# A metaformer on one core: which engine empties PSUM in the spectral stage, where its forward transform stands, and how the inverse over blocks is laid out

## The chip, the core and the metric

The kernel runs on one core of a Trainium2 chip. The core's engines work in parallel and are joined by semaphores: TensorE (PE, which multiplies matrices and loads its weights in a row of its own, PEld), VectorE (DVE), ScalarE (ACT), GpSimd (POOL) and SyncE (SP), which issues all DMAs of this kernel. TensorE writes to PSUM, a small memory; DVE or ACT must copy results from there to SBUF, the on-chip working memory, before the PSUM tile can be filled again. The metric is the device time of one execution in microseconds (us).

## The reference, cut to what matters

The model has two layers. Layer 0 is a selective scan in four directions and a soft mixture of experts, layer 1 a sum over rows and columns and a spectral filter. Only the end of layer 1, the spectral filter, is touched by the change.

```python
x = x + _L0_conv_ref(_ln_c(x), ...)            # selective scan, 4 directions
t = t + _L0_ffn_ref(_ln_t(t), ...)             # experts
x = x + _L1_conv_ref(_ln_c(x), Wself, Wm, Wk)
t = t + _L1_ffn_ref(_ln_t(t), sigma, phi, M_u, M_phi_plus, M_phi_minus, log_weights, gumbel)

def _stu_conv(phi, u, n):                      # n = 8192, u: (4, 4096, 128), phi: (4096, 16)
    Vf = jnp.fft.rfft(phi, n=n, axis=0)
    Uf_p = jnp.fft.rfft(u, n=n, axis=1)
    Uf_m = jnp.fft.rfft(u * sgn3, n=n, axis=1)
    U_plus = jnp.fft.irfft(Vf[None, :, :, None] * Uf_p[:, :, None, :], n=n, axis=1)[:, :sl]
    U_minus = jnp.fft.irfft(Vf[None, :, :, None] * Uf_m[:, :, None, :], n=n, axis=1)[:, :sl]
    return U_plus, U_minus * sgn[None, :, None, None]

out = jnp.einsum('btkd,k,kde->bte', U_plus, s, Mpp)
out = out + jnp.einsum('btkd,k,kde->bte', U_minus, s, Mpm)
```

The filter is a causal convolution of each of the 128 channels with 16 filters, followed by a mixing of channels; per frequency this is one 128 x 128 complex matrix, made from the 16 filters' spectra. The result is scaled by a weight per segment of the sequence and added to x.

## The kernel before

**Stages.** `tile_metaformer_kernel` runs a long main phase (the scans, with the other work dealt out between them), then the last experts, and then in sequence `to_slots(B - 1)`, `spectrum()` and `endings()`. The change lies in the last two, with small parts in the constants (`_dft_constants`) and in `filters`.

**The transform in two levels.** The sequence of 4096 is cut into NB = 64 blocks of BP = 64. A first transform over the blocks (`to_slots`) leaves NQ = 64 slots q in the memory tensor `ud`. `spectrum()` works on slots, FB = 2 of them in each of n = 32 rounds, and leaves `zd`, laid out [q, r, p, b, c] with r for real and imaginary part, p the place in the block and b the batch. `endings()` takes the inverse over the blocks and adds it to the residual, `x3_d`.

**One round of `spectrum()`.** Its parts, in the program's words:

- `load(i)` fetches the filters' spectra `vt`, the slots `u1` and the twiddle factors `fq`. `load_back(i)` fetches the product's result of the round before from memory (`zq`) with factors `gq`.
- `forward(i)`, line 1468: for each of the two slots, four matmuls into one half of a PSUM tile (L1474), then one copy of that half to `ut`.
- `taps_of(i)`, line 1486, the making: 16 steps j. Each fills two PSUM tiles of two banks with eight matmuls (L1495) on four row groups of 32, and copies each tile to `wt`, a tile that exists only once (`bufs=1`) (L1506 and L1509).
- `product(i)`, line 1513: 128 matmuls of `wt` with `ut` (L1524), eight PSUM tiles, eight copies to `zs`, which DMAs carry to `zf` in memory.
- `backward(i)`, line 1553: four matmuls of `zq` with `gq` (L1559), one copy to `zo`, two DMAs to `zd`.

All parts take their PSUM tiles from one pool of four (`banks()`), each of two banks. The loop over rounds is:

```python
forward(0)
for i in range(n):
    if i + 2 < n: load(i + 2)
    if i + 1 < n: between[0] = lambda: forward(i + 1)
    if i >= 1:    load_back(i - 1); between[C // 8 - 1] = lambda: backward(i - 1)
    taps_of(i, between)
    product(i)
```

So the forward of the next round stands behind step 0 of a making, the backward of the last behind step 15. An engine's instructions run in the order in which the build leaves them; near the seams of a round the build interleaves neighbouring parts (making instructions stand between the two halves of a forward, and a `zs` copy of the product may stand behind the first `wt` copy).

**Who copies.** `copy()` and `out()` (L1451, L1455) give every copy from PSUM in turn to ACT and DVE, by a counter that runs through all rounds. A round has 43 copies: 32 of `wt`, 2 of `ut`, 8 of `zs`, 1 of `zo`. As 43 is odd, the first copy of a making is ACT's in one round and DVE's in the next.

**`endings()`.** 16 groups g of four places p. `load_x` brings x3 into `xr3`, [64 blocks, 4 places, batch, channel], one DMA for each batch entry; `load` brings `zb`, [128, 4, 512], in two DMAs of 64 partitions; `turn` has four matmuls with the constant `gi_t` (128 x 64) into [64, 512] of PSUM (L1612), and for each a DVE operation that multiplies by `wpj`, the weight of the block's segment, and adds x3 (L1614); `put` writes the group to the output by four DMAs. All are issued by SP in the order of the program's text, with four groups of x3 fetched ahead. `wpj` is made in `filters` from a table of segments, on 64 partitions.

Of the kernel before, what the change touches and what calls it, by code (L numbers as in the profile page):

```python
# [47 lines left out]
def _dft_constants():  # L48


    j, q = np.arange(NB)[:, None], np.arange(NQ)[None, :]
    th = 2 * np.pi / (2 * NB) * (j * q)
    one = (q == 0) & (j >= 0)
    alt = np.where(j % 2 == 0, 1.0, -1.0) * np.ones((1, NQ))
    co, si = np.cos(th), np.sin(th)
    fwd = np.stack([co, np.where(one, alt, -si)], 1)
    back = np.stack([np.where(one, 1.0, 2 * co), np.where(one, alt, -2 * si)], 1) / (2 * NB)
    gi = np.moveaxis(back, 0, 2)

    seg = np.zeros((NB, 4))  # L60
    for i in range(NB):
        seg[i, 0 if i < NB // 8 else 1 if i < NB // 4 else 2 if i < NB // 2 else 3] = 1.0
    r = fwd.reshape(NB, 2 * NQ), gi.reshape(2 * NQ, NB), seg
    return [np.ascontiguousarray(x.astype(np.float32)) for x in r]


# [35 lines left out]
def kernel(  # L102
# [115 lines left out]
    gq_d = nc.inline_tensor(gq_c, name="dft_out").ap()  # L218
    fu_t = wp.tile([NB, P], F32, name="fu_t")
    nc.sync.dma_start(fu_t, nc.inline_tensor(fu_c, name="dft_u").ap())  # L220
    gi_t = const.tile([P, NB], F32, name="gi_t")
    nc.sync.dma_start(gi_t, nc.inline_tensor(gi_c, name="dft_back").ap())
    wpj = const.tile([NB, 1], F32, name="wpj")

    eps5 = wp.tile([P, 1], F32, name="eps5")
    nc.vector.memset(eps5, 1e-5)
# [477 lines left out]
    def filters():  # L704

        with tc.tile_pool(name="fl", bufs=2) as fp:
# [30 lines left out]
            for s in range(2, -1, -1):  # L737
                nc.vector.tensor_add(
                    wseg[:, s : s + 1], wseg[:, s + 1 : s + 2], wt[:, 3 - s : 4 - s]
                )  # L740
            sg4 = fp.tile([NB, 4], F32, name="sg4")
            nc.sync.dma_start(sg4, nc.inline_tensor(seg_c, name="dft_seg").ap())
            nc.vector.tensor_mul(sg4, sg4, wseg[0:NB, :])
            nc.vector.reduce_sum(wpj, sg4, axis=AX.X)

            nc.scalar.activation(sg, sg, AF.Ln)
# [686 lines left out]
    def spectrum():  # L1433

        with tc.tile_pool(name="sp", bufs=2) as sp, tc.tile_pool(
# [7 lines left out]
                )  # L1443
            wt = sp.tile([P, C // 4, FB * 2 * BP, 4], F32, name="wt", bufs=1)
            u1, fq, vt, ut, zq, gq = {}, {}, {}, {}, {}, {}
            side["e"] = 0

            def banks():
                return sps.tile([P, 2, 512], F32, name="sp_ps", tag="ps")

            def copy():  # L1451
                side["e"] += 1
                return nc.scalar.copy if side["e"] % 2 else nc.vector.tensor_copy

            def out(dst, src):  # L1455
                copy()(dst, src)  # L1456

            def load(i):
                vt[i] = sp.tile([P, FB, 2 * BP], F32, name="vt")
# [8 lines left out]
            def forward(i):  # L1468
                ps = banks()
                ut[i] = sp.tile([P, FB, BP, 2, B], F32, name="ut")  # L1470
                for s in range(FB):
                    q = FB * i + s
                    for b in range(B):
                        nc.tensor.matmul(  # L1474
                            ps[:, s, b * 2 * BP : (b + 1) * 2 * BP],
                            u1[q][:, b, :],
                            fq[q],
                            start=True,
                            stop=True,
                        )  # L1480
                    out(
                        ut[i][:, s].rearrange("d m u b -> d b (m u)"),
                        ps[:, s].rearrange("d (b n) -> d b n", b=B),
                    )

            def taps_of(i, between):
                for j in range(C // 8):
                    pair = [banks(), banks()]
                    for t in range(2):
                        for g in range(4):  # L1490
                            rows = slice(g * KK, (g + 1) * KK)
                            bank = pair[g // 2][:, g % 2]
                            woven = bank.rearrange("d (n t) -> d t n", t=2)[:, t]
                            plain = bank[:, t * 256 : (t + 1) * 256]
                            nc.tensor.matmul(  # L1495
                                woven if (g // 2 + j) % 2 else plain,
                                taps[rows, j, t, :],
                                vt[i][rows].rearrange("k s n -> k (s n)"),
                                start=True,
                                stop=True,  # L1500
                            )
                    for h in range(2):
                        dst = wt[:, 2 * j + h]
                        if (h + j) % 2:
                            src = pair[h].rearrange("d g (n t) -> d n g t", t=2)
                            copy()(dst.rearrange("d n (g t) -> d n g t", g=2), src)  # L1506
                        else:
                            src = pair[h].rearrange("d g (t n) -> d n (g t)", t=2)
                            copy()(dst, src)  # L1509
                    if j in between:  # L1510
                        between[j]()

# [55 lines left out]
            n = NQ // FB  # L1568
            load(0)
            load(1)  # L1570
            forward(0)
            for i in range(n):
                between = {}
                if i + 2 < n:
                    load(i + 2)
                if i + 1 < n:
                    between[0] = lambda: forward(i + 1)
                if i >= 1:
                    load_back(i - 1)
                    between[C // 8 - 1] = lambda: backward(i - 1)  # L1580
# [4 lines left out]

    def endings():

        with tc.tile_pool(name="gi", bufs=3) as gp, tc.tile_pool(
            name="gi_ps", bufs=8, space=PSUM
        ) as gps:  # L1590
            zb, xr = {}, {}

            def mine(t, b, g):
                return t[b].rearrange("(j p) c -> j p c", j=NB)[:, 4 * g : 4 * g + 4, :]

            def load_x(g):
                xr[g] = gp.tile([NB, 4, B, C], F32, name="xr3", bufs=6)
                for b in range(B):
                    nc.sync.dma_start(xr[g][:, :, b, :], mine(x3_d, b, g))  # L1599

            def load(g):
                zb[g] = gp.tile([P, 4, B * C], F32, name="zb", bufs=4)
                for r in range(2):
                    nc.sync.dma_start(
                        zb[g][r * NQ : (r + 1) * NQ],
                        zd[:, r, 4 * g : 4 * g + 4].rearrange("q p b c -> q p (b c)"),
                    )

            def turn(g):
                for t in range(4):  # L1610
                    ps = gps.tile([NB, B * C], F32, name="gi_ps", tag="ps")
                    nc.tensor.matmul(ps, gi_t, zb[g][:, t, :], start=True, stop=True)  # L1612
                    xt = xr[g][:, t].rearrange("j b c -> j (b c)")
                    nc.vector.scalar_tensor_tensor(xt, ps, wpj, xt, ALU.mult, ALU.add)  # L1614

            def put(g):
                for b in range(B):
                    nc.sync.dma_start(mine(out, b, g), xr[g][:, :, b, :])

            for g in range(4):  # L1620
                load_x(g)
            n = BP // 4
            for g in range(n + 3):
                if g + 4 < n:
                    load_x(g + 4)
                if g < n:
                    load(g)
                if 0 <= g - 2 < n:
                    turn(g - 2)
                if 0 <= g - 3 < n:  # L1630
                    put(g - 3)

    def run(pieces):
        for _ in pieces:
# [352 lines left out]
```

## Time and profile before

| What | Time |
|---|---|
| Median of 3 runs | 10265.2 us (10250.67 to 10266.36) |
| The profiled execution itself | 10262.52 us |
| Span of its trace, first to last instruction | 10260.5 us |
| Mean granted TensorE clock | 0.814 of full speed |
| Main phase and last experts, up to the start of `to_slots` | about 8693 us |
| `to_slots`, tables and start of `spectrum()` | about 8693 to 8757 us |
| `spectrum()`, to the issue of its last DMA | to about 10099 us |
| `endings()`, first load to the end | 10101.5 to 10260.5 us |

The profile is of one execution. The page gives each engine's busy time and the costliest groups of instructions over the whole span; the chain of waits is the work that ended last, followed back from the end; the timeline shows instructions in order of time (start, duration, engine, line, operation, how many were merged into the line, and in brackets the idle time of the engine before them and what ended it). Windows give each engine's busy time within a stretch, TensorE's granted clock, the busy share of the 16 DMA engines and the bytes moved per second. A share somewhat above 1 comes from packets that overlap.

### The profile page before, as it was taken

How to read it: one execution, taken by the hardware profiler on the slowest of the kernel's cores; microseconds unless marked ns; L12 is line 12 of the kernel's file. 1: busy time of each engine (PE TensorE's matmuls, PEld its weight loads, DVE VectorE, ACT ScalarE, POOL GpSimd, SP SyncE). 2: the span in 40 equal slices, each digit the busy share in tenths (PEclk: the TensorE clock that was granted, in tenths of full speed). 3: DMA queues.
4: the chain of work that ended last, by engine and by line, in shares of the span. 5: the costliest groups of instructions: out<-in, count | busy, mean ns of one | idle time of the engine just before them, and what ended most of it. 6: DMA issues, size and time to landing. Idle time of an engine off the chain costs nothing. (4 is left out here: it accounts for less than half of the span.)

```text
span 10260.5 us, 137964 instructions
## 1 busy us (share of the span) xinstructions
PE 7621.4 (74%) x45570; PEld 4890.3 (48%) x45570; DVE 8536.1 (83%) x7103; ACT 6160.7 (60%) x11847; POOL 6493.8 (63%) x5948
## 2 busy tenths in 40 slices
PE   7676776667667767677767776767777667899996
PEld 3444444444543545444544554543555445555552
DVE  0899999989999999998999999999999961566663
ACT  4665766656755466676765576765576653455551
POOL 1677787877877778887877788877778751000000
PEclk9788787767877878788868887868877777999998
DMA  2556556657656645656847656856646664333336
GB/s 89 167 172 205 179 182 216 190 180 219 202 167 202 220 154 171 203 182 198 252 163 225 214 158 206 239 161 222 220 158 195 196 183 134 94 88 90 90 89 162
DMA packets 941919, 1806.04 MB, mean 176 GB/s; under 512 B 88184, under 2 KB 506648, under 8 KB 937624
## 3 DMA queue, kind: packets, MB, share of 16 engines
q1 hardware_dynamic: 941208, 1797.22, 56.5%
q8 instruction: 366, 6.00, 0.2%
q14 instruction: 345, 2.83, 0.1%
HBM read 1554.66 MB, written 242.22 MB: 175 GB/s over the span
## 5 line engine op out<-in xcount | busy, mean ns | idle before, releaser
L1846 POOL TENSOR_TENSOR hh<-hh,bc 128x1024 f32<-128x1024 f32 x2048 | 4888.7, 2387 | 387.3 <-DVE hh L1836 152.7
L1836 DVE TENSOR_TENSOR_SCAN hh<-da,hst,db 128x512 f32<-128x512 f32 x3584 | 4392.6, 1267 | 285.3 <-PE y L1872 31.0
L1872 PE MATMUL y<-ident,hh 128*128 128x128 f32 x16384 | 2716.0, 320 | 1530.3 <-POOL hh L1846 1432.6
L1786 ACT ACTIVATE da<-dl,aneg 128x512 f32<-128x512 f32 x4096 | 2783.0, 717 | 1560.3 <-DVE hh L1836 1547.5
L1872 PEld LDWEIGHTS y<-ident,hh 128*128 128x128 f32 x16384 | 2250.2, 165 | 2493.3 <-POOL hh L1846 1867.2
L1830 DVE TENSOR_TENSOR db<-du,bc 128x1024 f32<-128x1024 f32 x1920 | 2365.1, 1232 | 108.3 <-ACT du L1767 28.2
L1845 POOL COPY hst<-hh 128x2 f32<-128x2 f32 x1792 | 365.6, 204 | 1052.9 <-DVE hh L1836 922.0
L1495 PE MATMUL sp_ps<-vt,taps 32*128 32x256 f32 x8192 | 630.5, 409 | 17.9 <-DVE wt L1506 6.3
L1836 DVE TENSOR_TENSOR_SCAN hh<-da,db 128x512 f32<-128x512 f32 x512 | 597.0, 1208 | 38.5 <-PE y L1872 5.8
L440 PE MATMUL cv_ps<-xh,diag 128*128 128x512 f32 x1152 | 525.1, 598 | 1.7 <-ACT sg_v L382 0.9
L1495 PEld LDWEIGHTS sp_ps<-vt,taps 32*128 32x128 f32 x8192 | 426.7, 186 | 204.4 <-DVE wt L1506 78.8
L1524 PE MATMUL sp_ps<-wt,ut 128*32 128x256 f32 x8192 | 448.7, 379 | 1.4 <-DVE wt L1509 1.4
L1830 DVE TENSOR_TENSOR db<-dx,bc 128x1024 f32<-128x1024 f32 x128 | 175.7, 1373 | 298.8 <-POOL dx L1714 287.4
L1686 PE MATMUL dt_ps<-dts,dtw 8*128 8x512 f32 x512 | 380.1, 846 | 51.3 <-ACT sg_v L382 34.5
L1711 PE MATMUL dl_ps<-ex,ident 128*128 128x512 f32 x512 | 321.6, 717 | 127.5 <-POOL ex L1705 127.5
L1506 DVE COPY wt<-sp_ps 128x1024 f32<-128x1024 f32 x256 | 313.3, 1224 | 106.6 <-PE sp_ps L1495 93.1
L1509 DVE COPY wt<-sp_ps 128x1024 f32<-128x1024 f32 x256 | 313.0, 1223 | 79.2 <-PE sp_ps L1495 76.3
L1456 DVE COPY zs<-sp_ps 128x1024 f32<-128x1024 f32 x128 | 156.5, 1222 | 254.2 <-PE sp_ps L1524 252.0
L1705 POOL TENSOR_TENSOR ex<-ex,dx 128x1024 f32<-128x1024 f32 x128 | 301.8, 2358 | 103.9 <-DMA bc<-bc_d 72.9
L1524 PEld LDWEIGHTS sp_ps<-wt,ut 128*32 128x32 f32 x8192 | 264.7, 110 | 193.9 <-issue 23.5
L1509 ACT COPY wt<-sp_ps 128x1024 f32<-128x1024 f32 x256 | 259.1, 1012 | 147.5 <-PE sp_ps L1495 145.5
L1714 POOL TENSOR_TENSOR dx<-dl,xc 128x1024 f32<-128x1024 f32 x128 | 302.5, 2364 | 64.4 <-ACT dl L1712 56.5
(289 smaller groups left out, 9915.7 us busy)
## 6 DMA issues: line engine op xcount, KB each, us to landing
bc<-bc_d SPq DMA_DIRECT2D x2048, 512.0 KB
xc<-xc_d SPq DMA_DIRECT2D x128, 512.0 KB
y_d<-ys SPq DMA_DIRECT2D x128, 512.0 KB
w1t<-in_w_dram SPq DMA_DIRECT2D x96, 512.0 KB
w2t<-in_w_dram SPq DMA_DIRECT2D x192, 256.0 KB
xc_x<-xc_d SPq DMA_DIRECT2D x64, 512.0 KB
yk<-y_d SPq DMA_DIRECT2D x128, 256.0 KB
yk<-y_d SPq DMA_DIRECT2D x256, 128.0 KB
```

The lines of the kernel that those rows point to most:

```text
L440: nc.tensor.matmul(ps, diag[:, h, t, :], xh[:, 8 * g + dy : 8 * g + dy + 8, dx : dx + W], start=(t == 0), stop=(t == 8),)
L1495: nc.tensor.matmul(woven if (g // 2 + j) % 2 else plain, taps[rows, j, t, :], vt[i][rows].rearrange("k s n -> k (s n)"), start=True, stop= ...
L1509: copy()(dst, src)
L1524: nc.tensor.matmul(ps[32 * g : 32 * g + 32, k // 2, (k % 2) * 256 :][:, 0:256], w0.rearrange("d m u b -> d (m u b)"), wt[:, :, n : n + 2, ...
L1686: nc.tensor.matmul(ps, dtw[:, k, h * P : (h + 1) * P], dts, start=True, stop=True)
L1711: nc.tensor.matmul(ps, ident, t[:, h], start=t is dl, stop=t is w)
L1786: i_act = nc.scalar.activation(das[t][:, h, :], sizes[t // N][0][:, h, :], AF.Exp, scale=aneg[:, tk, h, t % N : t % N + 1],)
L1830: nc.vector.tensor_mul(db, src, bcs[s][:, 0:1, :].to_broadcast([P, 2, SC]))
L1836: i_dve = nc.vector.tensor_tensor_scan(o, d0, d1, init, ALU.mult, ALU.add)
L1845: nc.gpsimd.tensor_copy(hsts[t // N][:, :, t % N], hhs[t][:, :, last])
L1846: i_pool = nc.gpsimd.tensor_mul(hhs[t], hhs[t], bcs.pop(t)[:, 1:2, :].to_broadcast([P, 2, SC]))
L1872: i_pe = nc.tensor.matmul(ys[c][:, q, h, :], hhs[t][:, h, q * P : (q + 1) * P], ident, is_transpose=True, start=(n == 0 and k > 0 and q % ...
```

## The change

There are three parts.

1. **Choice of the copying engine.** In place of the counter, `copy(on_act, on_dve)` keeps a running sum of copy times for each engine and gives a copy to ACT if ACT's sum with it is not above DVE's. The times written into the program are 1.01 for ACT and 1.22 for DVE, and 1.06 on both for `ut`. Both sums are set to zero at the start of each round.
2. **Forward in front of the making.** `forward(i + 1)` is called ahead of `taps_of(i)`, no longer behind step 0.
3. **Inverse over blocks on 128 partitions.** The place p is split into its half h, a group g (now 8) and four places t, and block and half make one index of 128. `gi_t` becomes two matrices of 128 x 128 with zeros woven in, so that two accumulating matmuls, one for each half, fill [128, 512] of PSUM. `xr3` is laid out [128, batch, 4, channel], `zb` [128, 2, 4, 512]; `wpj` and its table have 128 rows. The pool of this stage is opened with `reuse_waits="tile"`, by which a tile waits for what held its own memory before and not for the release of a whole pool. Three groups are fetched ahead; for each group the turn comes first, then the loads for three groups later, then the put.

```diff
-    seg = np.zeros((NB, 4))
+    seg = np.zeros((NB, 2, 4))
     for i in range(NB):
-        seg[i, 0 if i < NB // 8 else 1 if i < NB // 4 else 2 if i < NB // 2 else 3] = 1.0
-    r = fwd.reshape(NB, 2 * NQ), gi.reshape(2 * NQ, NB), seg
+        seg[i, :, 0 if i < NB // 8 else 1 if i < NB // 4 else 2 if i < NB // 2 else 3] = 1.0
+    r = fwd.reshape(NB, 2 * NQ), np.zeros((2 * NQ, 2, NB, 2)), seg.reshape(P, 4)
+    for h in range(2):
+        r[1][:, h, :, h] = gi.reshape(2 * NQ, NB)
...
-    gi_t = const.tile([P, NB], F32, name="gi_t")
-    nc.sync.dma_start(gi_t, nc.inline_tensor(gi_c, name="dft_back").ap())
-    wpj = const.tile([NB, 1], F32, name="wpj")
+    gi_t = const.tile([P, 2, P], F32, name="gi_t")
+    nc.sync.dma_start(
+        gi_t, nc.inline_tensor(gi_c.reshape(P, 2, P), name="dft_back").ap()
+    )
+    wpj = const.tile([P, 1], F32, name="wpj")
...
-            sg4 = fp.tile([NB, 4], F32, name="sg4")
+            sg4 = fp.tile([P, 4], F32, name="sg4")
...
-            nc.vector.tensor_mul(sg4, sg4, wseg[0:NB, :])
+            nc.vector.tensor_mul(sg4, sg4, wseg)
...
-            def copy():
-                side["e"] += 1
-                return nc.scalar.copy if side["e"] % 2 else nc.vector.tensor_copy
-
-            def out(dst, src):
-                copy()(dst, src)
+            def copy(on_act, on_dve):
+                a, d = busy["act"] + on_act, busy["dve"] + on_dve
+                if a <= d:
+                    busy["act"] = a
+                    return nc.scalar.copy
+                busy["dve"] = d
+                return nc.vector.tensor_copy
+
+            def out(dst, src, on_act=1.01, on_dve=1.22):
+                copy(on_act, on_dve)(dst, src)
...
             load(0)
             load(1)
+            busy.update(act=0.0, dve=0.0)
             forward(0)
             for i in range(n):
                 between = {}
                 if i + 2 < n:
                     load(i + 2)
+                busy.update(act=0.0, dve=0.0)
                 if i + 1 < n:
-                    between[0] = lambda: forward(i + 1)
+                    forward(i + 1)
...
-        with tc.tile_pool(name="gi", bufs=3) as gp, tc.tile_pool(
+        with tc.tile_pool(name="gi", bufs=3, reuse_waits="tile") as gp, tc.tile_pool(
...
             def mine(t, b, g):
-                return t[b].rearrange("(j p) c -> j p c", j=NB)[:, 4 * g : 4 * g + 4, :]
+                return t[b].rearrange("(jh g t) c -> g jh t c", jh=P, t=4)[g]
 
             def load_x(g):
-                xr[g] = gp.tile([NB, 4, B, C], F32, name="xr3", bufs=6)
+                xr[g] = gp.tile([P, B, 4, C], F32, name="xr3", bufs=6)
                 for b in range(B):
-                    nc.sync.dma_start(xr[g][:, :, b, :], mine(x3_d, b, g))
+                    nc.sync.dma_start(xr[g][:, b], mine(x3_d, b, g))
 
             def load(g):
-                zb[g] = gp.tile([P, 4, B * C], F32, name="zb", bufs=4)
+                zb[g] = gp.tile([P, 2, 4, B * C], F32, name="zb", bufs=4)
                 for r in range(2):
                     nc.sync.dma_start(
                         zb[g][r * NQ : (r + 1) * NQ],
-                        zd[:, r, 4 * g : 4 * g + 4].rearrange("q p b c -> q p (b c)"),
+                        zd[:, r].rearrange("q (h g t) b c -> g q h t (b c)", h=2, t=4)[g],
                     )
 
             def turn(g):
                 for t in range(4):
-                    ps = gps.tile([NB, B * C], F32, name="gi_ps", tag="ps")
-                    nc.tensor.matmul(ps, gi_t, zb[g][:, t, :], start=True, stop=True)
-                    xt = xr[g][:, t].rearrange("j b c -> j (b c)")
+                    ps = gps.tile([P, B, C], F32, name="gi_ps", tag="ps")
+                    for h in range(2):
+                        nc.tensor.matmul(
+                            ps, gi_t[:, h, :], zb[g][:, h, t, :], start=(h == 0), stop=(h == 1)
+                        )
+                    xt = xr[g][:, :, t, :]
                     nc.vector.scalar_tensor_tensor(xt, ps, wpj, xt, ALU.mult, ALU.add)
 
             def put(g):
                 for b in range(B):
-                    nc.sync.dma_start(mine(out, b, g), xr[g][:, :, b, :])
-
-            for g in range(4):
+                    nc.sync.dma_start(mine(out, b, g), xr[g][:, b])
+
+            n = BP // 8
+            for g in range(3):
+                load(g)
                 load_x(g)
-            n = BP // 4
-            for g in range(n + 3):
-                if g + 4 < n:
-                    load_x(g + 4)
-                if g < n:
-                    load(g)
-                if 0 <= g - 2 < n:
-                    turn(g - 2)
-                if 0 <= g - 3 < n:
-                    put(g - 3)
+            for g in range(n):
+                turn(g)
+                if g + 3 < n:
+                    load(g + 3)
+                    load_x(g + 3)
+                put(g)
```

In the diff, `taps_of` calls `out(dst, src)` where it called `copy()(dst, src)`, and the copies of `forward` pass 1.06 for both engines.

More of the change, by code (lines that the diff above doesn't have):

```diff
@@ L1445, in spectrum @@
             u1, fq, vt, ut, zq, gq = {}, {}, {}, {}, {}, {}
-            side["e"] = 0
+            busy = {}
             def banks():
                 return sps.tile([P, 2, 512], F32, name="sp_ps", tag="ps")
-            def copy():
-                side["e"] += 1
-                return nc.scalar.copy if side["e"] % 2 else nc.vector.tensor_copy
-            def out(dst, src):
-                copy()(dst, src)
+            def copy(on_act, on_dve):
[7 more added lines that the diff above has]
+                copy(on_act, on_dve)(dst, src)
             def load(i):
@@ L1483, in forward @@
                         ps[:, s].rearrange("d (b n) -> d b n", b=B),
+                        1.06,
+                        1.06,
                     )
@@ L1505, in taps_of @@
                             src = pair[h].rearrange("d g (n t) -> d n g t", t=2)
-                            copy()(dst.rearrange("d n (g t) -> d n g t", g=2), src)
+                            out(dst.rearrange("d n (g t) -> d n g t", g=2), src)
                         else:
                             src = pair[h].rearrange("d g (t n) -> d n (g t)", t=2)
-                            copy()(dst, src)
+                            out(dst, src)
                     if j in between:
```

## The prediction

> **What bounds the kernel now.** I read the page first, then the chain of waits in order of time from 8690 us on, because every edit but two tiny ones lies there: the order of the built program shows no difference on any engine before the spectral stage, apart from a larger constant load and two 64- against 128-partition instructions in the filters.
>
> ```profile
> span 10260.5 us, 137964 instructions
> ...
> PE 13%; DVE 2%; DMA 1%; ACT 1%; issue 1%; SPq 0%; POOL 0%; POOLq 0%; DVEq 0%; ACTq 0%
> ```
>
> The chain in order of time gives the rounds of the spectral stage (start, duration, work). The long piece at L1524 is a round's product, so its starts are the period:
>
> ```profile
> 8945.19 13.95 PE sp_ps L1524 x256
> ...
> 8986.68 13.95 PE sp_ps L1524 x256
> ...
> 9028.17 13.95 PE sp_ps L1524 x256
> ...
> 9069.65 13.95 PE sp_ps L1524 x256
> ...
> 9088.30 2.08 PE sp_ps L1474 x8
> ```
>
> The next product starts at 9112.45: three rounds of 41.49 and one of 42.80, mean 41.82, 32 rounds. The long one holds a forward half (L1474) of 2.08 us, elsewhere 1.17. The timeline of a making (L1495) in full swing:
>
> ```profile
> 9432.33 2.28 PE L1495 MATMUL sp_ps<-vt,taps 32*128 32x256 f32 x32 [0.18 <-DVE wt L1506]
> ...
> 9433.51 1.22 DVE L1506 COPY wt<-sp_ps 128x1024 f32<-128x1024 f32 x1
> 9433.57 1.01 ACT L1509 COPY wt<-sp_ps 128x1024 f32<-128x1024 f32 x1 [0.32 <-PE sp_ps L1495]
> 9434.65 1.22 DVE L1509 COPY wt<-sp_ps 128x1024 f32<-128x1024 f32 x1
> ...
> 9434.79 2.28 PE L1495 MATMUL sp_ps<-vt,taps 32*128 32x256 f32 x32 [0.18 <-DVE wt L1506]
> ```
>
> Two steps j take 2.46 us, and this is a loop of latencies, not a sum of copies: a bank freed by DVE at 9434.73 lets PE go on at 9434.79; 12 instructions later (71 ns each, the last lasting 0.374) the bank is full, at 9435.95; DVE copies it from 9435.97 to 9437.19; PE goes on. The four tiles hold two steps, so every second step waits for this loop, whichever engine has more work in sum.
>
> The last 159 us (10101.5 to 10260.5) are the inverse over blocks. Windows: time, then PE, PEld, DVE, ACT, POOL busy, granted clock, DMA share, GB/s. First x3 loads alone, then a stretch of steady state:
>
> ```profile
> 10105.00:10110.00 5.00, 0.00 (x0) 0.00 (x0) 0.00 (x0) 0.00 (x0) 0.00 (x0) 0.50 0.95 186
> 10110.00:10115.00 5.00, 0.00 (x0) 0.00 (x0) 0.00 (x0) 0.00 (x0) 0.00 (x0) 0.50 1.25 178
> ...
> 10160.00:10190.00 30.00, 16.65 (x25) 4.45 (x26) 8.92 (x12) 0.00 (x0) 0.00 (x0) 0.79 0.86 222
> ```
>
> DMA is full or nearly so while PE is half idle. Compare the expert weights, whose packets are 2 KB:
>
> ```profile
> 8490.00:8500.00 10.00, 10.00 (x163) 9.84 (x160) 0.00 (x0) 0.00 (x0) 0.00 (x0) 0.95 1.05 386
> ```
>
> Same full share, twice the bytes. The reason is in the packets of the last stretch:
>
> ```profile
> DMA packets 37581, 33.95 MB, mean 212 GB/s; under 512 B 2592, under 2 KB 35360, under 8 KB 35529
> ```
>
> 32,768 of them are 512 B: `xr3` is laid out [j, p, b, c], so a row of 2 KB in memory falls into four pieces on chip.
>
> [...]512 B packets move 182 GB/s at a full share, 2 KB packets 386[...] an L1612 instruction goes every 0.86 us after a wait and every 0.43 later, the clock reading 0.50 and 1.00[...].
>
> **The change, part by part.**
>
> *Choice of engine.* The sums 1.01 (ACT) and 1.22 (DVE) put 18 of the 32 `wt` copies on ACT and 14 on DVE where it was 16 and 16 (built order). Mostly they still alternate, so each pair of steps still has a DVE copy in its loop and stays at 2.46 us: gain nothing, though DVE gets 2.4 us less work a round. Twice a step has both copies on ACT: step 4, and step 15. At step 4 the second bank is freed after 1.01 + 0.91 instead of 1.22, that is 0.7 later; with the slack of 0.18 in the loop I take +0.5, bounds 0 and +0.9. At step 15 the backward's 3.63 us of PE hide it. The loop of PE alone would be 2.28; that is the most to be had, 8 x 0.18 = 1.4 a round.
>
> *Forward in front of the making.* Before (round at 9460.88): step 0, a wait of 1.10, forward half, a wait of 0.52 for `ut`, second half, step 1; step 2 begins 6.94 after the product. After, in the built order: half one (0 to 1.20), its copy on ACT (to 2.26), four making instructions meanwhile, half two (2.30 to 3.50; it writes the same tile, so it waits for that copy), its copy on DVE (to 4.56), now ahead of the last `zs` copy there (to 5.80). Step 0's second bank takes the forward's tile and waits until 4.60; step 1's second bank waits for that `zs`, 5.84, and needs 12 instructions: step 2 at 6.69. One wait is exchanged for another; gain 0.25. ACT holds, as before, the `zs` copy behind step 0's `wt` copy; it ends at 5.95, before step 2 needs the bank. The `u1` and `fq` loads on SP follow the forward and have a round's time; no SP wait becomes late.
>
> Round: 6.69 + 16.97 (steps 2 to 15, from 9467.82 to 9484.79) + 0.5 + 3.63 + 13.95 = 41.74 without a slow half, 42.07 with one in four. Against 41.82 over 31 rounds: -2.5 or +7.8; I take the middle, +3. The first round pays about 2 more, one DMA latency: forward(1) now stands in front of the first making and its `u1` tiles come free only after forward(0). Spectral stage: **+5**, from -5 to +20.
>
> *Inverse on 128 partitions.* Half the turns (32) with two accumulating matmuls each: PE keeps 128 instructions of 0.43 us, 55 us at full clock, 110 at half. DVE has 32 operations of 0.74 instead of 64: 24 us off, all of it beside DMA, worth nothing itself. DMA: x3 and out now move 2 KB runs on both sides. Before, 159 us x 0.90 = 143 us of full share; 32,768 packets at 45 ns over 16 engines (182 GB/s) are 92 of it, which leaves 51 for the 16.8 MB of `zb` (8 KB packets). After: 16.8 MB at 387 = 43, plus 51: 94. One group is then 6.4 (`zb`) + 2.7 (x3) + 2.7 (out). `zb` of group 0 is issued on SP first and, as x3 did before, when the last `zd` has landed, at T0 = 10101.5 by the old clock. Loads 0 to 7 and puts 0 to 3 precede the last load: 83.6 + 2 latency; its `zb` lands 2.7 before the last x3, at T0 + 83; turn 7 takes 7, DVE's last 0.5, the put with issue and landing 4.7: T0 + 95. The old stage ran 6% behind its DMA sum (9.45 a group against 8.9), so T0 + 101. Against T0 + 159: **-58**. Bounds: all at 387 and no gap, T0 + 88 (-71); PE at half clock throughout, 8 x 13.7 behind a first `zb` at 8.4, T0 + 123 (-36). `reuse_waits="tile"` frees x3's loads from the release of the whole pool, but SP stands at `zb` 0 before them: nothing. The larger constant is 0.1 MB more at 387 GB/s, 0.3 us during setup.
>
> *Sum.* Profiled execution 10262.5 (span 10260.5 and 2 around it): 10262.5 + 5 - 58 = 10209.5. The median of the runs is 2.7 higher: **10212**.
>
> **The rivals.**
> - *A, the forecast*: 10212, own range 10190 to 10234. Chance 0.68.
> - *B, PE's clock bounds the ending*: before, turns ran at 0.86 an instruction for half of the time. For: each turn waits for `zb`. Against: the new groups have 16 instructions on all 128 columns, 6.9 of 11.8 us busy. 10262.5 + 5 - 36 + 2.7 = 10234. Chance 0.12.
> - *C, the packets don't speed up*: the 182 GB/s would come from the strided rows in HBM, not from the 512 B pieces. Against: the rows were 2 KB in memory before too. 143 us of DMA stay, -8: 10262. Chance 0.06.
> - *D, slower: the clock drops in every round.* Place: the new gaps of 0.85 and 0.93 us around the second forward half, right behind the product. Price: with half one, half two and steps 0 and 1 slow, about 2.6 a round (twice the 1.31 of the one in four), 83 in all: 10295. It decides from 58/32 = 1.8 us a round. Against: the old gaps of 1.10 and 0.52 were as long in sum. Chance 0.07.
> - *E, the balance does free the making*: PE's own 2.28 a pair; 1.4 x 32 = 45 more: 10167. For: PE's recorded wait is on DVE alone. Against: the loop above. Chance 0.07.
>
> About 0.2% (20 us) is what a measurement can tell here. Faster: A nearly whole (0.66), B two thirds (0.09), E (0.07): 0.83 rounded up for A's low tail; slower: D, 0.07; between: 0.10. B reaches 10234 and some beyond, so 10187 to 10248 leaves out C, D, E.
>
> **What would show it.** The product's starts in the chain stay 41.4 to 42.1 apart; making lines still show two steps in 2.46 with waits on DVE and one longer wait on ACT near step 4; DVE's `wt` copies number 448. From the last `zd` to the end about 100 us, DMA share near 1 with over 330 GB/s, hardly a packet between 512 B and 2 KB. Wrong if the rounds leave 41 to 42.5, if the ending's bytes stay near 220 GB/s, or if its turns go at 0.86 an instruction throughout.

## The result, and the profile after

| | Before | After |
|---|---|---|
| Median of 11 runs each | 10264.31 us (10250.67 to 10280.63) | 10238.56 us (10228.4 to 10251.68) |
| Ratio of after to before | | 0.9975, 95% interval 0.9966 to 0.9984 |
| The profiled execution | 10262.52 us | 10238.56 us |
| Main phase, up to the first `ub` load of the spectral stage | 8694.55 us | 8703.29 us |
| From there to the first product | 81.6 us | 81.4 us |
| First product to last product (31 rounds) | 1294.6 us | 1292.6 us |
| Last product to the first load of `endings()` | 30.7 us | 31.3 us |
| First load of `endings()` to the end of the span | 159.0 us | 128.2 us |

The change is faster by 0.25%, 25.7 us in the medians. The forecast was 53 us. In the two profiles the stages differ by +8.7, -0.2, -2.0, +0.6 and -30.8, in sum -23.7. The first figure is no effect of the change: over the thirteen profiles of the study this phase, in which the kernels hardly differ, ended anywhere from 8678.6 to 8705.2, whichever kernel it was. What the change moved is the last stage, and it moved it by 31 us where 58 were forecast.

The page of after, span and the chain's shares by engine:

```profile
span 10236.8 us, 137678 instructions
...
PE 13%; DMA 2%; ACT 2%; DVE 1%; issue 0%; POOL 0%; SPq 0%; POOLq 0%; DVEq 0%; ACTq 0%
```

DMA's share of the chain rose from 1% to 2%: in the last stage the chain now runs through transfers up to the last turn. The chain of waits of after in the spectral stage, in order of time (start, duration, work):

```profile
8826.42 13.95 PE sp_ps L1534 x256
...
8850.68 1.94 ACT wt L1464 x2
...
8868.05 13.95 PE sp_ps L1534 x256
...
8909.69 13.95 PE sp_ps L1534 x256
```

The rounds are 41.63 and 41.64 (before 41.49), and the piece in the middle is the step whose two `wt` copies both went to ACT, as the forecast said. Over 31 rounds the mean is 41.70 against 41.76: after has only four rounds with the long forward half, before had about one in four.

The chain of after in the last stage:

```profile
10110.54 11.97 DMA xr<-x_d
...
10122.53 14.67 DMA xr<-x_d
...
10137.21 22.47 DMA zb<-zd
...
10159.69 6.33 DMA out_dram<-xr
...
10221.40 9.37 PE gi_ps L1625 x16
```

Up to 10221 us every long piece is a transfer; TensorE and VectorE come in only with the last turn, which takes 9.4 us where the forecast had 7. So the stage is bound by DMA, as forecast, but by slower DMA than forecast. This is the DMA view of after over that stage, its GB/s in 40 equal slices of 3.2 us, and its packets:

```profile
GB/s 74 239 208 198 372 203 208 198 366 203 211 204 360 203 218 204 394 325 206 218 227 398 311 226 199 265 404 262 236 196 341 406 211 236 209 398 407 348 165 165
DMA packets 11539, 33.60 MB, mean 260 GB/s; under 512 B 1291, under 2 KB 1291, under 8 KB 9488
```

The 512 B packets are gone, and the rate has two levels: near 400 and near 205. The windows of after (time, then PE, PEld, DVE, ACT, POOL busy, granted clock, DMA share, GB/s) say which transfers belong to which level:

```profile
10115.00:10120.00 5.00, 0.00 (x0) 0.00 (x0) 0.00 (x0) 0.00 (x0) 0.00 (x0) 0.50 0.99 204
...
10150.00:10180.00 30.00, 19.06 (x35) 7.69 (x34) 6.68 (x9) 0.00 (x0) 0.00 (x0) 0.78 1.03 271
...
10220.00:10230.00 10.00, 8.60 (x15) 3.82 (x16) 2.25 (x3) 0.00 (x0) 0.00 (x0) 0.70 1.03 383
```

In the first window the `zb` loads of the first group run, in the last there are 2 KB packets alone, most of them of the output. All three have a full share, 0.99 to 1.03, and move 204, 271 and 383 GB/s: a share of 1 says that every engine holds a packet; it doesn't say how fast the packets move. Here 8 KB packets into 64 partitions move at 204 GB/s, about half the 383 of 2 KB packets from 128.

### The profile page after: what moved, and what is told of

Its sections match the earlier page's. It is cut to its first block, busy times and chain, and to the rows that moved or that the text cites. A ratio compares the mean times of both kernels' runs of the same rounds, so it can differ in the third digit from the quotient of the medians.

```text
span 10236.8 us, 137678 instructions
## 1 busy us (share of the span) xinstructions
PE 7657.0 (75%) x45570; PEld 4946.3 (48%) x45570; DVE 8452.8 (83%) x7022; ACT 6198.1 (61%) x11896; POOL 6492.4 (63%) x5948
## 5 line engine op out<-in xcount | busy, mean ns | idle before, releaser
L1464 ACT COPY wt<-sp_ps 128x1024 f32<-128x1024 f32 x576 | 570.4, 1014 | 158.5 <-PE sp_ps L1505 139.8
L1464 DVE COPY wt<-sp_ps 128x1024 f32<-128x1024 f32 x448 | 531.3, 1220 | 71.6 <-PE sp_ps L1505 58.3
L1505 PEld LDWEIGHTS sp_ps<-vt,taps 32*128 32x128 f32 x8192 | 453.5, 186 | 218.3 <-DVE wt L1464 116.2
L1725 ACT COPY dl<-dl_ps 128x512 f32<-128x512 f32 x256 | 147.8, 578 | 329.0 <-PE dl_ps L1724 328.8
```

The source lines that it names most:

```text
L1464: copy(on_act, on_dve)(dst, src)
L1505: nc.tensor.matmul(woven if (g // 2 + j) % 2 else plain, taps[rows, j, t, :], vt[i][rows].rearrange("k s n -> k (s n)"), start=True, stop= ...
```

## The experiments

Two theories for the last stage. **H**: a transfer that touches only partitions 0 to 63, or only 64 to 127, moves at half rate, whatever its packets; the change brought x3 and the output to 128 partitions, and `zb` is still loaded by two DMAs of 64. **P**, the forecast's own reading: packets of 512 B move at half the rate of packets of 2 KB and more. For the spectral stage: does the running sum gain or lose, and does the forward in front? "The ending" below is the time from the first load of `endings()` to the end of the span in the profiled execution.

| Run | Made from | Ending | Clean round | Time, and ratio to before with its 95% interval |
|---|---|---|---|---|
| before | | 159.0 | 41.49 | |
| after | | 128.2 | 41.64 | 10238.56, 0.9975 (0.9966 to 0.9984) |
| e1_before_x2k | before | 147.6 | 41.49 | 10256.56, 0.9998 (0.9989 to 1.0006) |
| e2_after_x512 | after | 137.1 | 41.63 | 10245.18, 0.9983 (0.9976 to 0.9989) |
| e3_after_zb128 | after | 87.6 | 41.63 | 10191.35, 0.9936 (0.9920 to 0.9953) |
| e8_zb128_x512 | e3 | 98.8 | 41.63 | 10207.36, 0.9948 (0.9931 to 0.9964) |
| e9_zb64_rows | e3 | 127.3 | 41.63 | 10237.75, one run |
| e10_zb64_spread | e3 | 88.8 | 41.63 | 10204.46, one run |
| e11_before_x2k_two | e1 | 155.6 | 41.49 | 10254.43, one run |
| e4_spec_both | before | 156.6 | 41.63 | 10264.7, 1.0003 (0.9994 to 1.0012) |
| e5_spec_balance | before | 157.5 | 41.44 | 10262.96, one run |
| e6_spec_forward | before | 157.2 | 41.39 and 41.67 | 10265.89, one run |
| e7_zb128_alternate | e3 | 90.1 | 41.39 and 41.68 | 10191.29, 0.9933 (0.9918 to 0.9948) |

### The last stage: packets or partitions

**Only the packets, on 64 partitions (e1_before_x2k).** The kernel before, with 2 KB runs of x3 and output, still on 64 partitions:

```diff
-                xr[g] = gp.tile([NB, 4, B, C], F32, name="xr3", bufs=6)
+                xr[g] = gp.tile([NB, B, 4, C], F32, name="xr3", bufs=6)
                 for b in range(B):
-                    nc.sync.dma_start(xr[g][:, :, b, :], mine(x3_d, b, g))
+                    nc.sync.dma_start(xr[g][:, b], mine(x3_d, b, g))
```

> The kernel before with one thing changed: xr3 laid out [64 blocks, batch, 4 places, channel], so that x3 loads and output stores move 2 KB runs instead of four of 512 B, still on 64 partitions; nothing is left out. Theory P (packets of 512 B were what held the DMA at 182 GB/s, as in the prediction): the stretch of x3 loads alone runs at 350 to 390 GB/s and the last stage, from the landing of the last zd to the end, falls from 159 us to 100 to 112; in all about 50 us faster. Theory H (a DMA that touches only 64 partitions runs at half rate, whatever its packets): x3 loads stay at 170 to 215 GB/s, the last stage at 150 to 162 us, in all within 10 us of before.

Measured: ending 147.6, which is 11 below before and far from P's value, though a little below H's lower end. A window of this kernel while x3 alone is loaded:

```profile
10120.00:10125.00 5.00, 0.00 (x0) 0.00 (x0) 0.00 (x0) 0.00 (x0) 0.00 (x0) 0.50 0.67 205
```

205 GB/s looks like H's half rate, but the share is 0.67: SyncE issued 20 of these DMAs in 12.63 us, 0.63 us for each 128 KB, and that alone allows no more than 208 GB/s. So the time of the stage speaks against P, while this rate decides nothing. A later run (e11) takes the issue out of the way.

**Only the packets, on 128 partitions (e2_after_x512).** The kernel after, with `xr3` as [128, place, batch, channel], so that its rows fall into 512 B pieces again:

```diff
-                xr[g] = gp.tile([P, B, 4, C], F32, name="xr3", bufs=6)
+                xr[g] = gp.tile([P, 4, B, C], F32, name="xr3", bufs=6)
                 for b in range(B):
-                    nc.sync.dma_start(xr[g][:, b], mine(x3_d, b, g))
+                    nc.sync.dma_start(xr[g][:, :, b, :], mine(x3_d, b, g))
```

> The kernel after with one thing changed: xr3 laid out [128, 4 places, batch, channel], so that x3 loads and output stores move 512 B pieces on 128 partitions; nothing is left out. Theory P: the stores fall back to about 180 GB/s and the last stage grows from 128 us by 45 to 50. Theory H: the stores at the end stay at 350 GB/s or more and the last stage at 126 to 133 us.

Measured: ending 137.1, 8.9 us above after; H's range was missed by 4 us, P's increase by far more. A window of this kernel behind the last `zb` load, in which only 512 B packets run, to be set beside the 383 GB/s of after:

```profile
10235.00:10245.00 10.00, 6.96 (x15) 2.71 (x13) 3.00 (x4) 0.00 (x0) 0.00 (x0) 0.91 1.11 323
```

512 B packets on 128 partitions move at 323 GB/s here. The 182 GB/s of the forecast were therefore for the most part not the price of the packets.

**`zb` in loads of 128 partitions (e3_after_zb128).** The kernel after, with each `zb` load taking one half h on all partitions; the partition index becomes (q, r), and the constant's rows stand in that order:

```diff
-        r[1][:, h, :, h] = gi.reshape(2 * NQ, NB)
+        r[1][:, h, :, h] = gi.transpose(1, 0, 2).reshape(2 * NQ, NB)
...
-                for r in range(2):
+                for h in range(2):
                     nc.sync.dma_start(
-                        zb[g][r * NQ : (r + 1) * NQ],
-                        zd[:, r].rearrange("q (h g t) b c -> g q h t (b c)", h=2, t=4)[g],
+                        zb[g][:, h],
+                        zd.rearrange("q r (h g t) b c -> h g (q r) t (b c)", h=2, t=4)[h, g],
                     )
```

> The kernel after with zb loaded in DMAs of 128 partitions (slot and real or imaginary part as one index, the constant's rows permuted to match) instead of 64 and 64; the same bytes, the same 8 KB packets, the same number of DMAs, nothing is left out. Theory H: zb takes 43 us of DMA instead of about 82, the last stage falls from 128 to 86 to 98 us, in all 30 to 42 us faster than after. Theory P, with zb at 329 GB/s and some other loss: the last stage stays at 122 to 130.

Measured: ending 87.6, 40.6 below after. The DMA view of this kernel over the last stage, 40 slices of 2.2 us, and its packets:

```profile
GB/s 85 391 413 335 319 422 415 403 429 417 398 412 423 398 385 403 397 319 398 395 405 418 398 405 397 412 429 411 389 399 434 422 408 390 405 404 406 405 351 28
DMA packets 11546, 33.61 MB, mean 382 GB/s; under 512 B 1296, under 2 KB 1296, under 8 KB 9495
```

Bytes and packets are those of after, and the level near 205 has gone. Added up by their recorded times over the 16 engines, the packets of `zb` took 41.5 us here and 76.7 us in after, those of x3 and the output 44.2 and 49.3. But the edit changed two things at once: the partitions of a load, and the distance of its rows in memory, 128 KB where it was 256 KB.

**The two taken apart (e9_zb64_rows, e10_zb64_spread).** Both start from e3. The first loads partitions 0 to 63 and 64 to 127 apart again, but with rows 128 KB apart:

```diff
-                for h in range(2):
+                for k in range(2):
                     nc.sync.dma_start(
-                        zb[g][:, h],
-                        zd.rearrange("q r (h g t) b c -> h g (q r) t (b c)", h=2, t=4)[h, g],
+                        zb[g][k * NQ : (k + 1) * NQ],
+                        zd.rearrange("q r (h g t) b c -> g (q r) h t (b c)", h=2, t=4)[
+                            g, k * NQ : (k + 1) * NQ
+                        ],
                     )
```

> The kernel of the 87.6 us ending (zb in two loads of 128 partitions), with zb loaded again in two loads of 64 partitions, 0 to 63 and 64 to 127, but each taking neighbouring rows of zd (128 KB apart) where the kernel after takes every second row (256 KB apart). Bytes, packets and number of loads stay. Theory H, a load that writes only one half of the partitions moves at half rate: ending 122 to 134 us, as after (128.2), and 195 to 215 GB/s while zb is loaded alone. Rival S, the distance of the rows in memory made zb slow: ending 85 to 98 us, near 400 GB/s.

The second loads rows 256 KB apart, as after, into 64 partitions that lie in both halves, every second one:

```diff
-                for h in range(2):
+                for r in range(2):
                     nc.sync.dma_start(
-                        zb[g][:, h],
-                        zd.rearrange("q r (h g t) b c -> h g (q r) t (b c)", h=2, t=4)[h, g],
+                        zb[g][r::2],
+                        zd[:, r].rearrange("q (h g t) b c -> g q h t (b c)", h=2, t=4)[g],
                     )
```

> As the kernel of the 87.6 us ending, but each zb load again takes every second row of zd (256 KB apart), as the kernel after, and writes 64 partitions: every second one of the 128, so both halves. H (the half of the partitions decides): ending 85 to 98 us. Rival S (distance of the rows): 122 to 134 us. Rival N (a load of 64 partitions is slow wherever they lie): 122 to 134 us here, and 122 to 134 in the run with neighbouring rows too.

Measured: endings of 127.3 and 88.8. The DMA view of the run with neighbouring rows (e9), in 40 slices of 3.2 us:

```profile
GB/s 259 218 212 195 366 205 218 194 367 205 212 199 367 205 215 198 389 348 207 218 205 394 330 225 206 246 403 287 230 193 286 415 240 230 186 348 407 407 241 185
```

and the same view of the run with spread partitions (e10), in slices of 2.25 us:

```profile
GB/s 41 342 426 335 341 413 428 390 431 426 383 414 422 403 388 402 406 328 397 402 404 406 353 396 403 408 402 390 387 402 420 368 393 383 406 405 406 371 336 9
```

The first repeats after's two levels, the second has only the upper one. While `zb` is loaded at the start of the stage, e9 moves 202 GB/s (10115 to 10120 us) and e10 404 (10116 to 10121). So it is neither the distance of the rows nor the number of partitions in a load, but that a load lies in one half of them: H is shown for `zb`. Why the half counts shows in none of the traces.

**x3 on 64 partitions, with issue out of the way (e11_before_x2k_two).** As e1, with ScalarE issuing every second x3 load:

```diff
-                    nc.sync.dma_start(xr[g][:, b], mine(x3_d, b, g))
+                    e = nc.scalar if b % 2 else nc.sync
+                    e.dma_start(xr[g][:, b], mine(x3_d, b, g))
```

> The kernel before with 2 KB runs of x3 on 64 partitions, its x3 loads issued in turn by SyncE and ScalarE, so that the issue (0.63 us for each 128 KB from one queue, 208 GB/s) no longer holds them. H: the first x3 loads, alone, stay at 200 to 215 GB/s and the DMA share rises from 0.67 to 0.95 or more. Rival P (2 KB packets move at 386 wherever they go): 300 to 390 GB/s. Ending 140 to 150 us under H, 125 to 142 under P.

Two windows of this kernel while x3 is loaded (alone up to 10110.6 us, from where on `zb` packets run beside it):

```profile
10102.00:10107.00 5.00, 0.00 (x0) 0.00 (x0) 0.00 (x0) 0.00 (x0) 0.00 (x0) 0.50 1.08 200
10107.00:10112.00 5.00, 0.00 (x0) 0.00 (x0) 0.00 (x0) 0.00 (x0) 0.00 (x0) 0.50 1.11 208
```

2 KB packets into 64 partitions: 200 to 208 GB/s at a full share. Before had 178 to 186 with 512 B packets in the same place. P is out for x3 too. The ending, 155.6, lies outside both ranges; issuing from two queues made it 8 us longer than in e1, and why was not followed up.

**512 B packets beside fast `zb` loads (e8_zb128_x512).** e3 with e2's edit:

> The kernel after with zb loaded on 128 partitions, and x3 and output moved in 512 B pieces on 128 partitions: the price of packet size alone, with no DMA confined to 64 partitions; nothing is left out. Theory P: 45 ns a packet, so 49 us more than the 87.6 us of zb on 128 partitions alone. Theory H: 512 B packets cost little once all partitions are reached; by the 9 us that they cost beside the slow zb, the last stage is 92 to 102 us.

Measured: ending 98.8, 11.2 above e3. Its DMA view over the last stage has a mean of 342 GB/s, where e3 has 382. Together with e1 (11.4 less) and e2 (8.9 more) the packets' own price is 9 to 11 us, wherever it was looked for.

### The spectral stage

**Both parts alone (e4_spec_both).** The kernel before with the running sums and the forward in front, and the old last stage.

> The kernel before with the first two parts of the change only (choice of engine, forward in front); the last stage as before; nothing is left out. The prediction's loop of latencies: rounds of 41.64 us mostly, as in the trace of after, the last stage 159, in all 0 to 8 us faster than before. If the main phase moved by the 9 us seen between the two traces because of the change's constants, its start of the slots' transform is at about 8694 here; if it is only spread between executions, it may lie anywhere from 8685 to 8710.

Measured: ratio 1.0003, interval 0.9994 to 1.0012; clean rounds 41.63, in the mean of all 31 rounds 41.84 (before 41.76; over the stage 2.6 us more). The main phase ended at 8700, between the two profiles of before and after, so it follows no part of the change. The two parts together are worth nothing that can be measured.

**The running sums alone (e5_spec_balance).** The kernel before, with the diff's `copy` and `out` and the sums set to zero in each round; the forward stays behind step 0.

> The kernel before with the choice of engine by running sums alone; the forward stays behind step 0, the last stage is as before; nothing is left out. Loop of latencies (two steps need a fill, one DVE copy and two handovers, however the sums stand; a step with both copies on ACT costs 0.3 to 0.8 us more): rounds without a slow forward half are 41.5 to 42.3 us. Balance theory (DVE's sum was the bound): rounds of 40.0 to 40.6.

The chain of this kernel, two products and the step with both copies on ACT:

```profile
9406.59 13.95 PE sp_ps L1530 x256
...
9430.66 1.94 ACT wt L1460 x2
...
9448.03 13.95 PE sp_ps L1530 x256
```

Rounds of 41.44, just under the range of 41.5 and more, and nowhere near the 40.0 to 40.6 that a balance that frees the making would give. VectorE's smaller sum buys 0.05 us a round: the making is a loop of latencies, and rival E is out. The step with two copies on ACT doesn't show the forecast's 0.5 either: if it costs anything, the rest of the round gains as much.

**The forward in front alone (e6_spec_forward).**

```diff
-                    between[0] = lambda: forward(i + 1)
+                    forward(i + 1)
```

> The kernel before with the forward in front of the making alone; copies still alternate; nothing is left out. Loop of latencies: one wait is exchanged for another, so the gain is the 0.25 us of the prediction, and no step has two ACT copies: rounds without a slow half are 41.0 to 41.4 us, 0.2 to 0.6 below the 41.64 with both parts. If the forward's place were worth more, 40.5 or less.

The chain of this kernel, three products in a row:

```profile
9368.19 13.95 PE sp_ps L1524 x256
...
9409.86 13.95 PE sp_ps L1524 x256
...
9451.26 13.95 PE sp_ps L1524 x256
```

Rounds of 41.67 and 41.40 in turn: one kind 0.1 under before, the other 0.2 over it, 0.04 over it in the mean. The expected 41.0 to 41.4 was missed in every second round. The alternation fits the 43 copies of a round, by which each engine gets the first copy in every second round; with sums that start at zero in each round (e4, after) all clean rounds are alike. It was not tested further.

**The best ending with the old alternation (e7_zb128_alternate).** e3 with the counter in `copy`.

> The kernel after with zb loaded on 128 partitions and with copies alternating as before in place of the running sums; nothing is left out. Last stage as with zb on 128 partitions alone, 86 to 90 us; rounds 0.2 to 0.6 us shorter than 41.64 where no half is slow, so in all 0 to 20 us faster than zb on 128 partitions alone (10191), and the fastest of these kernels.

Measured: 10191.29, where e3 has 10191.35; clean rounds 41.39 and 41.68 in turn. The expected gain over e3 didn't come: every second round is 0.05 us longer than e3's, and the running sums could be left out without loss. e3 and e7 are faster than both kernels of the study: 0.9936 and 0.9933 of before, that is 69 and 65 us below the runs of before taken beside them, where after is 26 below its own.

## Why the prediction was right or wrong

**The step that failed: the DMA sum of the last stage**, "16.8 MB at 387 = 43, plus 51: 94", and in it the 51 us for `zb`. They were a remainder: 143 us of full share in before, less 92 for x3 and the output. The traces hold each packet's size and time. Added up by size and divided by 16 engines, as the DMA share is, they give (us; packets of 4 B, up to 2 us, stand only in the sum):

| | x3 and output | `zb` | All packets | Stage |
|---|---|---|---|---|
| before, as the forecast split it | 92 | 51 | 143 | 159 |
| before, trace | 68.5 | 71.8 | 142.4 | 159.0 |
| e1, trace | 54.2 | 69.5 | 125.6 | 147.6 |
| after, forecast | 43 | 51 | 94 | 101 |
| after, trace | 49.3 | 76.7 | 126.9 | 128.2 |
| e3, trace | 44.2 | 41.5 | 86.4 | 87.6 |

The 92 came from 45 ns a packet, read where x3 is loaded alone; over the whole stage before's 512 B packets took 33 ns in the mean. What the forecast gave them too much was missing from `zb`. In after `zb` took 76.7 where 51 were put down, x3 and the output 49.3 for 43: 33 us in all. The stage missed by 27, because the 7 us that the forecast added for gaps were only 1.3. Recorded times can overlap (before's share is 1.25 in the window from 10110 us), so the split is read from the traces and was not varied by itself.

Before's own trace showed the rate of `zb`. In these two windows (columns as above) all data packets are 8 KB ones of `zb`:

```profile
10126.00:10131.00 5.00, 4.19 (x6) 0.92 (x4) 2.74 (x4) 0.00 (x0) 0.00 (x0) 0.66 1.00 210
10131.00:10136.00 5.00, 3.62 (x8) 1.01 (x8) 2.97 (x4) 0.00 (x0) 0.00 (x0) 1.00 1.00 211
```

At 210 GB/s the 16.8 MB are 80 us. Where `zb`, x3 and the output were under way together, before reached up to 300 GB/s, as its DMA view of the stage shows (slices of 4 us from 10101 us):

```profile
GB/s 99 188 178 178 213 195 227 199 229 216 237 200 266 168 305 128 208 244 184 299 165 242 201 210 272 162 283 176 220 226 209 285 166 249 253 293 262 221 62 84
```

So something ran side by side there, transfers of the upper half beside those of the lower or loads beside stores; no run separates the two, though in after two loads into the two halves together kept to 204 to 218 GB/s. Nor did a run time stores from 64 partitions alone: H is shown for the loads of `zb` and x3.

**What the 31 us were.** From e1 to after the packets' sum didn't fall (125.6 and 126.9), and the stage still went from 147.6 to 128.2. So x3 and the output on 128 partitions did not, in sum, shorten the DMA's work (`zb` lost what they gained); the engines stopped standing idle, 22 us of e1's stage and 1.3 of after's. In before SyncE waited 31.9 us at x3's loads for stores to land, in after 2.6. Larger packets account for 9 to 11 us of the 31 (e1, e2), the rest of part 3 for 19 to 22. Which of its pieces closed the gaps (fewer and larger DMAs, the order of issue, `reuse_waits="tile"`) was not taken apart.

Behind the failed step stands one wrong reading. Two rates, 182 and 386 GB/s, differed in the size of their packets and in the partitions that they touched, and the forecast named the packets. Their own price is 9 to 11 us, not 49. On 128 partitions 512 B packets alone move at 323 GB/s (e2) and 328 (e8, 10190 to 10200 us), where 2 KB and 8 KB packets together move 399 to 409 (e3, 10100 to 10120 and 10140 to 10160 us): not quite as fast, but far nearer to it than 182 made it look. Loading `zb` by halves of the partitions, and not on all 128, cost 40.6 us (after against e3).

With the measured -30.8 in place of -58, and -2 in place of +5 for the spectral stage, the forecast's own sum would be 10212 + 27 - 7 = 10232, against 10238.56; after's single executions spread from 10228 to 10252.

**Bounds and rivals.** The lower gain that the forecast allowed for the last stage, -36, came from TensorE at half clock, not from DMA, and -30.8 lies outside it. Rival C, that x3 and the output stay at 182 GB/s because of their rows in memory, is out: with the same 2 KB rows the output moves at 383. That `zb` would go on at about 210 GB/s stood on no list. The measured time lies near rival B's 10234, but not by B's mechanism: over 30 us of steady state after's DMA share is 1.03 while TensorE is 19.06 us busy, and in e3, where DMA moves 387 to 409 GB/s, TensorE's granted clock reads 1.00 (10100 to 10170 us). Rival D, a drop of the clock in each round, didn't come: after's clean rounds are 41.64 and only four of 31 are long. E fell by e5.

**The spectral stage**, +5 forecast (bounds -5 to +20), -2.0 in after's profile, +2.6 in e4's: inside the bounds. The -2.0 is partly luck: by its clean rounds alone after would be 31 x 0.14 = 4.3 us longer than before, and its few long rounds took that back. The 2 us put down for the first round didn't show: the first product starts 81.4 us into the stage, before 81.6. The structure was right, two of its terms were not, and their errors partly cancel. This is the timeline of after behind a product (which ends at 8840.37), with start, duration and in brackets the idle time before and what ended it:

```profile
8842.60 1.16 PE L1482 MATMUL sp_ps<-fq,u 128*128 128x128 f32 x8 [0.51 <-ACT ut L1464]
...
8843.87 1.06 DVE L1464 COPY ut<-sp_ps 128x512 f32<-128x512 f32 x1 [5.60 <-PE sp_ps L1482]
...
8844.78 1.20 DVE L1464 COPY zs<-sp_ps 128x1024 f32<-128x1024 f32 x1
...
8844.98 2.20 PE L1505 MATMUL sp_ps<-vt,taps 32*128 32x256 f32 x28 [0.59 <-DVE ut L1464]
...
8846.16 4.82 DVE L1464 COPY wt<-sp_ps 128x1024 f32<-128x1024 f32 x4 [0.18 <-PE sp_ps L1505]
...
8847.44 5.00 PE L1505 MATMUL sp_ps<-vt,taps 32*128 32x256 f32 x64 [0.26 <-DVE wt L1464]
```

Up to VectorE's copy of `ut` the forecast holds: as it said, the copy ends 4.56 us after the product. The forecast then let TensorE wait for the `zs` copy until 5.84 and put 12 instructions behind that, to 6.69. But behind the `zs` copy VectorE has a `wt` copy of the making as well: it starts at 5.79, ends at 7.02, and TensorE waits for it. By the chain's ends this wait is over 7.07 after the product, where the corresponding one of before, for `ut`, was over after 6.87: the forward in front costs 0.20 where a gain of 0.25 was put down. The rest of the making, with the step whose two copies are both ScalarE's, takes 16.98 where it took 17.04: for the forecast's +0.5 the trace has -0.06, so the loop has slack for it. In sum 41.63 where 41.74 was forecast. `wt` copies on VectorE number 448, as said.

**What stays open.** Why rounds with the long forward half are rarer in after's profile (4 of 31) than in e3's and e4's (9 or 10), which share its spectral stage and its clean rounds. No run shows what sets their number. This spread, with that of the main phase, is why single profiles are read here by stage.

## What to carry to other kernels

When two transfers differ in rate, list everything in which they differ, partitions too, before one difference is given the price; a run that changes one of them is cheap. A full DMA share says that the engines are occupied and nothing of bytes (in after 204 and 383 GB/s at shares of 0.99 and 1.03): look at GB/s beside it, and by kind of transfer, not as a remainder of an average. And try loading a tile of 128 partitions in pieces that each span both halves: cutting it along another axis, as e3 does, left bytes and packets as they were and took 40 us out of a stage of 128.

## What the runs showed of the hardware

- 64 partitions are not slow as such: loads into every second one of 128 moved at about 400 GB/s (e10), into 0 to 63 and then 64 to 127 at about 205 (e9), with the same bytes, packets and number of DMAs.
- Two loads from one queue, to the lower and then the upper half, did not add up in rate: the first group's pair of 1 MB loads in after kept to 204 to 218 GB/s from 10110 to 10120 us, though they were issued 0.66 us apart.
- A packet's size cost far less than the half of the partitions: 512 B packets alone on 128 partitions moved at 323 GB/s (e2), 2 KB packets into 0 to 63 at 200 (e11).
- Issuing DMAs of 128 KB from SyncE alone, at 0.63 us each, held a stretch at 205 to 207 GB/s at a share of 0.67 (e1, 10120 to 10130 us), by chance about the rate of `zb` on one half.
